# Cross-attention's scores laid out by key, their maxima taken from one turned block and handed round through DRAM

## The chip, the cores and the metric

The kernel runs on one core of a Trainium2 chip. A core has five engines that run their own instruction streams: TensorE (matrix products into PSUM, and transposes, which are products with an identity), VectorE, ScalarE, GpSimd and SyncE, which here only starts transfers. They share SBUF (128 partitions) and PSUM (eight banks of 2 KB per partition), and wait for each other through semaphores. The metric is device time in microseconds: the median of plain runs. The profile is of a separate, single execution of the same kernel.

## The reference

One decoder layer in float32: 32 sequences of 112 tokens, width 256, 16 heads of 16. Three residual steps: windowed causal self-attention, cross-attention to 375 context vectors with a bias that depends on the distance of key and query, and a mixture of eight experts of which each token takes two. The step that the change touches:

```python
q = (hidden_states @ Wq).reshape(B, S, H, D).transpose(0, 2, 1, 3)      # S = 112
kv = (key_value_states @ Wkv).reshape(B, K, 2, H, D)                    # K = 375
scores = jnp.einsum('bhsd,bhkd->bhsk', q, k)
rel = jnp.arange(K)[None, :] - jnp.arange(S)[:, None]
bias = rel_bias[_relative_position_bucket(rel)].transpose(2, 0, 1)[None]
attn = jax.nn.softmax(scores + bias, axis=-1)
out = jnp.einsum('bhsk,bhkd->bshd', attn, v).reshape(B, S, E)
return out @ Wo
```

The softmax subtracts each row's maximum over the 375 keys before the exponential. The sum that it divides by comes for free: the values carry a column of ones, so the product with the weights yields it too.

## The kernel before

**Slots.** Sequences go in eight groups of four. Everything up to the experts is cut into steps, and a table puts each step in a numbered slot. Slots 20 to 147 hold one cross item each, (group, sequence, quarter of the heads): four heads at a time, one per block of 32 partitions of the array. Slots 24 to 119 also hold one self item; the lead-in (slots 0 to 16) holds self items in pairs, and slots 120 to 147 cross items alone. The loop from line 1226 emits a slot: first `scores` of its item, then `average` of items three slots back, then `weigh` of the item two slots back, mixed with the steps due (projections of keys, values and queries, norms, routing), then the late ones (`divide`, `turn`, `attended`).

**Order.** `IN_ORDER` (line 51) names the engines whose instructions keep the written order: TensorE, VectorE, ScalarE. GpSimd's order is written out by `pool_order`. SyncE's is left to the scheduler. So an instruction that waits holds up all that is written behind it on its engine.

**One cross item.** `scores` (L464): per head block one product, queries as weights (32x112), keys moving (375 columns), into one of four PSUM banks (L477); self scores beside it (L488). VectorE adds the bias or mask and takes each row's minimum of the negated sum in the same instruction (L503, with a short read of the accumulator behind each). GpSimd subtracts the row's minimum (L509). `weigh` (L515), two slots later: twelve transposes (three chunks of 125 keys, four heads) bring the weights key-first (L530), and ScalarE takes the exponential out of PSUM (L531), one call per chunk. Self items take four transposes and one call. `average` (L533) multiplies by the values (L554). PSUM: four banks for scores, two for transposes, two for projections and the rest.

**Transfers.** SyncE loads each sequence's context (L434, two buffers, which at the start serve the bias table too: `hot` and `by_rel`), spreads the bias (L293 to L298: a small product, a store of `by_rel` to DRAM, and a load of 112 shifted copies), blanks the experts' row store in 28 pieces during the first 28 cross slots (L740, each held until that slot's scores are under way), stores results (L769) and loads x (L111). GpSimd starts the indirect transfers of the experts (L725, L962, L949, L1044). `first_plan` and `later_plan` (L909, L917) lay out the experts' tiles on VectorE, with small operations on tensors in SBUF such as L853 to L863.

Of the kernel before, what the change touches and what calls it, by code (L numbers as in the profile page):

```python
# [11 lines left out]
F32 = mybir.dt.float32  # L12
# [26 lines left out]
NWARM = 24  # L39
LAG = 4  # L40
# [10 lines left out]
IN_ORDER = {mybir.EngineType.PE, mybir.EngineType.DVE, mybir.EngineType.Activation}  # L51
# [27 lines left out]
def decoder_kernel(  # L79
# [95 lines left out]
    with ExitStack() as att, ExitStack() as own_att:  # L175
# [112 lines left out]
        bias = wpool.tile([S, H, K], F32, name="bias")  # L288

        def spread_bias():  # L290
# [6 lines left out]
            nc.sync.dma_start(by_rel_d, by_rel)  # L297
            nc.sync.dma_start(  # L298
                bias,
                bass.AP(  # L300
                    tensor=by_rel_d.tensor, offset=by_rel_d.offset,
                    ap=[[1, S], [NREL, H], [1, K]],
# [122 lines left out]
        def cross_queries(g, c):  # L425
            if c == 0:
                cross_q[g] = two.tile([P, NC2, 2, GT], F32, tag="q_cross", name=f"q_cross{g}")
            ps = ps_pj.tile([P, GT], F32, tag="pj", name=f"q2ps{g}_{c}")
            project(ps, wq_sb[:, :, c * P:(c + 1) * P], normed[g, 2][1])
            by_parity(cross_q[g][:, c], ps, g == 0)  # L430

        def load_context(g, b):
            ct = two.tile([P, NC2, K], F32, tag="ct", name=f"ct{g}_{b}")
            nc.sync.dma_start(ct, ctx_t[g * GB + b].rearrange("(c p) k -> p c k", p=P))  # L434
# [28 lines left out]

        def scores(cross, selfs):  # L464

            name = "_".join(str(v) for part in (cross or (), *selfs) for v in part)
            w = two.tile([S, 4, K + S], F32, tag="w", name=f"w{name}", bufs=3)
            low = small.tile([S, 3, 4], F32, tag="low", name=f"low{name}")
            at = K if cross else 0
            sc = [ps_sc.tile([S, 512], F32, tag="sc", name=f"sc{name}_{r}") for r in range(4)]  # L470
            if cross:
                g, b, s = cross
                c, p = divmod(s, 2)
                kT, q = keys[g, b][1], cross_q[g]
                for r in range(4):
                    rows = slice(32 * r, 32 * r + 32)
                    scored[cross] = nc.tensor.matmul(  # L477
                        sc[r][:, :K], q[rows, c, p, b * S:(b + 1) * S], kT[rows, c, :],
                        start=True, stop=True,
                    ).ins  # L480
            if selfs:
                g, b, s = selfs[0]
                c, p = divmod(s, 2)
                n, at_b = len(selfs), slice(b * S, (b + 1) * S)
                q, k = self_in[g, c]
                for r in range(4):
                    rows = slice(32 * r, 32 * r + 32)
                    nc.tensor.matmul(  # L488
                        sc[r][:, at:at + n * S].rearrange("q (p k) -> q p k", p=n),
                        q[rows, at_b], k[rows, p:p + n, at_b], start=True, stop=True,  # L490
                    )
            spans = []
            if cross:
# [831 lines left out]
```

## Time and profile before

| | us |
|---|---|
| median of plain runs (3 runs) | 1262.01 (1261.37 to 1262.40) |
| profiled execution, its own time | 1270.69 |
| span of that execution, first to last instruction | 1269.0 |
| first and last cross scores (L477) in it | 84.8 and 879.1 |
| TensorE busy in 300 to 400 us | 99.23 of 100 |
| VectorE, ScalarE, GpSimd busy there | 62.72, 54.10, 73.49 of 100 |

In a group line, the columns are line, engine, operation, output and inputs by name, shapes, count; after the first bar busy time in us and the mean ns of one; after the second the engine's idle time ahead of them and what ended it. In an order-of-time line: start and duration in us, then the instruction, a count where several follow without a gap (the duration then covers them all), and idle time before it in brackets. A transfer line ends with KB each and the median us from issue to landing. A float32 product is recorded as two instructions, a transpose as one. The table of stretches gives for each stretch its length and each engine's busy us.

### The profile page before, as it was taken

To read this page: it belongs to the slowest core of one execution; us is meant where nothing else is said; L and a number is where in the kernel's file an instruction comes from. 1 tells how busy PE (TensorE), PEld (TensorE's weight loads), DVE (VectorE), ACT (ScalarE), POOL (GpSimd) and SP (SyncE) were. 2 spreads that over 40 slices of the span, in tenths; PEclk is the share of its full clock that TensorE was granted. 3 is DMA by queue.
4 is the path that set the end of the run, shared out by engine and by line. 5 is a ranking of instruction groups with operands and counts; after the bars stand their busy time and mean duration, and the time that the engine had idled before them with its cause. 6 is when DMAs were issued, how large, how long until landed. Compare 5 with 4: busy or idle time off the path is not lost.

```text
span 1269.0 us, 29648 instructions
## 1 busy us (share of the span) xinstructions
PE 1227.4 (97%) x11648; PEld 972.5 (77%) x11648; DVE 651.0 (51%) x3012; ACT 570.1 (45%) x1201; POOL 839.0 (66%) x784
## 2 busy tenths in 40 slices
PE   9999999999999999999999999998789999999997
PEld 6666776777787787778778777766678898888886
DVE  5653654665566566557566665665325323332221
ACT  4454554555556456555555545454222222222222
POOL 8545664577767777767776796687556655665552
PEclk9999999999999999999999999999889999999999
DMA  8129876731100200200110020130366778888882
GB/s 229 34 69 197 203 169 161 180 87 42 44 26 14 73 14 14 74 24 15 39 33 26 14 59 26 36 128 25 115 209 195 212 208 276 239 234 244 244 247 30
DMA packets 70204, 143.00 MB, mean 113 GB/s; under 512 B 5521, under 2 KB 60498, under 8 KB 65074
## 3 DMA queue, kind: packets, MB, share of 16 engines
q0 software_dynamic: 20784, 85.92, 23.1%
q1 hardware_dynamic: 49282, 55.20, 17.3%
q8 instruction: 92, 1.51, 0.5%
q14 instruction: 46, 0.38, 0.1%
HBM read 90.88 MB, written 50.21 MB: 111 GB/s over the span
## 4 chain that ended last, share of the span: by engine, by line
PE 92%; ACT 2%; DVE 2%; POOL 1%; issue 1%; another core or an unknown queue 1%; DMA 0%; POOLq 0%; ACTq 0%; DVEq 0%
PE gu L1018 18%; PE wT L530 14%; PE py L1037 9%; PE sc L477 8%; PE k2ps L383 6%; PE v2ps L450 6%; PE avc_s L554 6%; PE ops L597 4%; PE ctrwT L530 3%; PE sc L488 3%; PE vps L416 2%; PE qps L383 2%; PE q2ps L383 2%; PE kps L383 2%; PE tp L377 1%; ACT wT L531 1%
## 5 line engine op out<-in xcount | busy, mean ns | idle before, releaser
L509 POOL TENSOR_TENSOR w<-w,low 112x448 f32<-112x448 f32 (+1 forms) x256 | 459.4, 1814 | 211.1 <-DVE low L503 210.1
L503 DVE CUSTOM_DVE_ANT_0 w<-sc,bias 112x375 f32<-112x375 f32 x512 | 270.4, 542 | 118.2 <-PE sc L488 96.2
L531 ACT ACTIVATE wT<-wT 125x448 f32<-125x448 f32 (+1 forms) x394 | 199.0, 542 | 100.7 <-PE wT L530 94.3
L1018 PE MATMUL gu<-xT,w 128*128 128x256 f32 (+1 forms) x1248 | 229.9, 342 | 1.9 <-issue 1.9
L530 PEld LDWEIGHTS wT<-ident,w 112*125 112x125 f32 (+1 forms) x1576 | 187.6, 174 | 46.1 <-issue 14.2
L1018 PEld LDWEIGHTS gu<-xT,w 128*128 128x128 f32 x1248 | 202.1, 192 | 26.8 <-issue 5.7
L530 PE MATMUL wT<-ident,w 112*125 112x112 f32 (+1 forms) x1576 | 216.0, 275 | 5.8 <-ACT wT L531 5.8
L1026 DVE SCALAR_TENSOR_TENSOR hid<-gu,w,sil 128x256 f32<-128x256 f32 (+1 forms) x156 | 67.2, 432 | 233.6 <-ACT sil L1023 228.2
L1044 POOL DMA_INDIRECT out_dram<-y,to x63 | 100.4, 1594 | 111.8 <-ACT y L1043 94.2
L1023 ACT ACTIVATE sil<-gu,w 128x256 f32<-128x256 f32 (+1 forms) x156 | 67.5, 433 | 147.4 <-PE gu L1018 131.9
L503 DVE CUSTOM_DVE_ANT_0 w<-sc,wmask 112x112 f32<-112x112 f32 x512 | 129.0, 268 | 2.6 <-PE sc L488 2.6
L477 PE MATMUL sc<-kT,q_cross 32*112 32x375 f32 x1024 | 123.3, 518 | 1.3 <-DVE low L503 1.0
L1037 PE MATMUL py<-w,hid 128*128 128x256 f32 x504 | 116.8, 383 | 0.4 <-DVE x L767 0.4
L1037 PEld LDWEIGHTS py<-w,hid 128*128 128x128 f32 x504 | 94.0, 193 | 12.1 <-DVE x L767 0.6
L450 PE MATMUL v2ps<-wkv_sb,ct 128*125 128x256 f32 x384 | 94.3, 381 | 0.0
L383 PE MATMUL k2ps<-ct,wkv_sb 128*128 128x375 f32 x256 | 92.3, 483 | 0.0
L503 DVE DVE_READ_ACCUMULATOR2_ANT low<- 112x1 f32 x1024 | 84.0, 82 | 0.0
L602 DVE TENSOR_TENSOR x<-x,ops 112x256 f32<-112x256 f32 x64 | 24.8, 418 | 111.1 <-PE ops L597 110.9
L1043 ACT ACTIVATE y<-py,gate 128x256 f32<-128x256 f32 x63 | 27.2, 471 | 108.6 <-PE py L1037 106.8
L725 POOL DMA_INDIRECT xslots<-xn,to x64 | 61.8, 966 | 19.7 <-issue 14.8
L962 POOL DMA_INDIRECT xg<-xslots,rows_i x63 | 60.7, 963 | 18.9 <-issue 17.4
L450 PEld LDWEIGHTS v2ps<-wkv_sb,ct 128*125 128x125 f32 x384 | 67.2, 188 | 7.7 <-DVE q_cross L389 0.5
(208 smaller groups left out, 1646.6 us busy)
## 6 DMA issues: line engine op xcount, KB each, us to landing
xslots<-zeros SPq DMA_DIRECT2D x28, 1060.0 KB, 7.6
ct<-in_ctx_t_dram SPq DMA_DIRECT2D x32, 375.0 KB, 3.3
x<-in_x_dram SPq DMA_DIRECT2D x8, 448.0 KB, 6.6
out_dram<-x SPq DMA_DIRECT2D x8, 448.0 KB, 3.2
bias<-by_rel_d SPq DMA_DIRECT2D x1, 2625.0 KB
xslots<-xn,to POOLq DMA_INDIRECT x64
xg<-xslots,rows_i POOLq DMA_INDIRECT x63
out_dram<-y,to POOLq DMA_INDIRECT x63
```

What stands on the lines that cost most here:

```text
L383: nc.tensor.matmul(ps, w[:, k, :], xT[:, k, :], start=(k == 0), stop=(k == NC2 - 1))
L450: nc.tensor.matmul(ps[:, i, :], ct[:, k, j * KC:(j + 1) * KC], wkv_sb[:, k, D:2 * D], start=(k == 0), stop=(k == NC2 - 1),)
L477: scored[cross] = nc.tensor.matmul(sc[r][:, :K], q[rows, c, p, b * S:(b + 1) * S], kT[rows, c, :], start=True, stop=True,).ins
L503: nc.vector.tensor_tensor_reduce(out=w[:, r, lo:hi], in0=sc[r][:, lo:hi], in1=add, scale=-1.0, scalar=FAR, op0=ALU.add, op1=ALU.min, accum ...
L509: nc.gpsimd.tensor_tensor(w[:, :, lo:hi], w[:, :, lo:hi], low[:, i].unsqueeze(2).to_broadcast([S, 4, hi - lo]), op=ALU.subtract,)
L530: nc.tensor.transpose(tp[:m, r, :], w[:, r, lo:lo + m], ident[:S, :S])
L531: nc.scalar.activation(wT[:m, j], tp[:m], AF.Exp, scale=-1.0)
L554: nc.tensor.matmul(av[32 * r:32 * r + 32, i, p, :], v, x, start=(j == 0), stop=(j == n - 1),)
L1018: nc.tensor.matmul(ps[:, m, :st], w[:, lo:lo + P], xT[:, c, :st], start=(c == 0), stop=(c == NC2 - 1),)
L1023: nc.scalar.activation(sil[:, :st], ps[:, 0, :st], AF.Silu, bias=w[:, bias_at + f:bias_at + f + 1])
L1037: nc.tensor.matmul(py[:, h, :], hid[:, f, h * P:(h + 1) * P], w[:, lo:lo + D], start=(f == 0), stop=(f == NFC - 1),)
L1044: added = nc.gpsimd.indirect_dma_start(out=out, out_offset=row_of(to[:, h:h + 1]), in_=y[:, h, :], in_offset=None, compute_op=ALU.add,)
```

## The change

Cross scores are computed transposed: keys as weights (three chunks of 32x125), queries moving (112 columns), twelve products instead of four. They come out key-first, in the layout in which `average` wants the weights, so the weights themselves are no longer transposed. The bias is loaded in the matching layout, 125 rows. VectorE adds it without taking a minimum.

The maximum over keys now runs across partitions. VectorE takes the larger of the three chunks, elementwise (`most`). At the head of the next slot `maxima` transposes that one block (four transposes), VectorE reduces it from PSUM to 112x4 maxima, SyncE stores these to DRAM and loads them back to all 125 partitions. A slot later `lessen` subtracts them on GpSimd, and a slot after that `exps` takes one exponential in place. Self items keep their way. `average` moves one slot later, except in the lead-in, and with it the last routing and plan.

Context loads and blanking stores go from SyncE's queue to ScalarE's. SyncE joins the engines in written order. Cross queries are held in one buffer per half of the width. Core of the diff:

```diff
-IN_ORDER = {mybir.EngineType.PE, mybir.EngineType.DVE, mybir.EngineType.Activation}
+IN_ORDER = {
+    mybir.EngineType.PE, mybir.EngineType.DVE, mybir.EngineType.Activation, mybir.EngineType.SP
+}
...
-        bias = wpool.tile([S, H, K], F32, name="bias")
+        bias = wpool.tile([KC, H, NKC, KC], F32, name="bias")
...
+            n = (NKC - 1) * KC + S
             nc.sync.dma_start(
-                bias,
+                bias.rearrange("k h j q -> k h (j q)")[:, :, :n],
                 bass.AP(
                     tensor=by_rel_d.tensor, offset=by_rel_d.offset,
-                    ap=[[1, S], [NREL, H], [1, K]],
+                    ap=[[1, KC], [NREL, H], [1, n]],
...
-            nc.sync.dma_start(ct, ctx_t[g * GB + b].rearrange("(c p) k -> p c k", p=P))
+            nc.scalar.dma_start(ct, ctx_t[g * GB + b].rearrange("(c p) k -> p c k", p=P))
...
-                for r in range(4):
-                    rows = slice(32 * r, 32 * r + 32)
-                    scored[cross] = nc.tensor.matmul(
-                        sc[r][:, :K], q[rows, c, p, b * S:(b + 1) * S], kT[rows, c, :],
-                        start=True, stop=True,
-                    ).ins
+                for j in range(NKC):
+                    for r in range(4):
+                        rows = slice(32 * r, 32 * r + 32)
+                        scored[cross] = nc.tensor.matmul(
+                            sc[r][:KC, j * S:(j + 1) * S], kT[rows, c, j * KC:(j + 1) * KC],
+                            q[rows, p, b * S:(b + 1) * S], start=True, stop=True,
+                        ).ins
...
             for r in range(4):
+                if cross:
+                    c, p = divmod(cross[2], 2)
+                    nc.vector.tensor_tensor(
+                        t[:, r], sc[r][:KC, :at].rearrange("k (j q) -> k j q", j=NKC),
+                        bias[:, 8 * c + 2 * r + p, :, :S], op=ALU.add,
+                    )
+                for i in range(n):
+                    lo = i * S
                     nc.vector.tensor_tensor_reduce(
-                        out=w[:, r, lo:hi], in0=sc[r][:, lo:hi], in1=add,
+                        out=w[:, r, lo:lo + S], in0=sc[r][:S, at + lo:at + lo + S], in1=wmask,
                         scale=-1.0, scalar=FAR, op0=ALU.add, op1=ALU.min,
                         accum_out=low[:, i, r:r + 1],
                     )
+            if cross:
+                most = two.tile([KC, 4, S], F32, tag="most", name=f"most{name}")
+                nc.vector.tensor_tensor(most, t[:, :, 0, :], t[:, :, 1, :], op=ALU.max)
+                nc.vector.tensor_tensor(most, most, t[:, :, 2, :], op=ALU.max)
+                shown[cross] = t, most
+            for i in range(n):
+                part = w[:, :, i * S:(i + 1) * S]
                 nc.gpsimd.tensor_tensor(
-                    w[:, :, lo:hi], w[:, :, lo:hi],
-                    low[:, i].unsqueeze(2).to_broadcast([S, 4, hi - lo]), op=ALU.subtract,
+                    part, part, low[:, i].unsqueeze(2).to_broadcast([S, 4, S]), op=ALU.subtract
                 )
...
+        def maxima(cross):
+            t, most = shown[cross]
+            name = "_".join(str(v) for v in cross)
+            tp = ps_tr.tile([S, 4, KC], F32, tag="tr", name=f"mtr{name}")
+            for r in range(4):
+                nc.tensor.transpose(tp[:, r, :], most[:, r, :], ident[:KC, :KC])
+            top = small.tile([S, 4], F32, tag="top_w", name=f"top_w{name}")
+            nc.vector.tensor_reduce(top, tp, AX.X, ALU.max)
+            top_d = dram.tile([4, S], F32, name=f"top_d{name}")
+            nc.sync.dma_start(top_d.rearrange("r q -> q r"), top)
+            spread = two.tile([KC, 4, S], F32, tag="spread", name=f"spread{name}")
+            nc.sync.dma_start(
+                spread.rearrange("k r q -> k (r q)"),
+                bass.AP(
+                    tensor=top_d.tensor, offset=top_d.offset, ap=[[0, KC], [1, 4 * S]],
+                ),
+            )
+            shown[cross] = t, spread
+
+        def lessen(cross):
+            t, spread = shown[cross]
+            nc.gpsimd.tensor_tensor(
+                t, t, spread.unsqueeze(2).to_broadcast([KC, 4, NKC, S]), op=ALU.subtract
+            )
+
+        def exps(cross):
+            t, _ = shown.pop(cross)
+            t = t.rearrange("k r j q -> k (r j q)")
+            nc.scalar.activation(t, t, AF.Exp)
...
-            filled = nc.sync.dma_start(part, zeros.unsqueeze(1).to_broadcast([P, n // P, ROW]))
+            filled = nc.scalar.dma_start(part, zeros.unsqueeze(1).to_broadcast([P, n // P, ROW]))
...
-                        slot = slot_of[kind, g, b, 2 * half + 1] + 3
+                        lead_in = kind == "s" and g < 2
+                        slot = slot_of[kind, g, b, 2 * half + 1] + (3 if lead_in else 4)
...
-        put_route(NG - 1, base[NG] + 5, base[NG] + 8)
-        free_self, free_all = base[NG - 1], base[NG] + 5
-        plan_at = {base[EARLY + 1] - 1: first_plan, base[NG] + 14: later_plan}
+        put_route(NG - 1, base[NG] + 6, base[NG] + 9)
+        free_self, free_all = base[NG - 1], base[NG] + 6
+        plan_at = {base[EARLY + 1] - 1: first_plan, base[NG] + 15: later_plan}
...
+                for i, fn in ((1, maxima), (2, lessen), (3, exps)):
+                    if cross := items.get(slot - i, (None,))[0]:
+                        do(partial(fn, cross))
                 if slot in items:
                     made[slot] = scores(*items[slot])
```

## The prediction

> **What bounds the kernel.** I read the page's totals first, then the stretch table, then the groups with shapes apart, then the order of time in one slot.
>
> ```profile
> PE 1227.4 (97%) x11648; PEld 972.5 (77%) x11648; DVE 651.0 (51%) x3012; ACT 570.1 (45%) x1201; POOL 839.0 (66%) x784
> ```
> ```profile
> core 0: us, PE busy (x) PEld busy (x) DVE busy (x) ACT busy (x) POOL busy (x), PEclk, DMA share, GB/s
> 300.00:400.00 100.00, 99.23 (x1165) 77.11 (x1165) 62.72 (x308) 54.10 (x112) 73.49 (x67) 1.00 0.11 32
> ```
>
> In attention TensorE has no gap (99.23 of 100), so removed TensorE work could pay in full. But VectorE is at 62.7 and GpSimd at 73.5 of 100, and the change gives VectorE more. The groups, mean ns second to last before the bar:
>
> ```profile
> L509 POOL TENSOR_TENSOR w<-w,low 112x1500 f32<-112x1500 f32 x128 | 344.7, 2693 | 207.1 <-DVE low L503 206.2 <-issue 0.5
> L503 DVE CUSTOM_DVE_ANT_0 w<-sc,bias 112x375 f32<-112x375 f32 x512 | 270.4, 542 | 118.2 <-PE sc L488 96.2 <-PE sc L477 17.0 <-issue 4.5
> ...
> L530 PE MATMUL wT<-ident,w 112*125 112x112 f32 x1152 | 166.7, 281 | 5.8 <-ACT wT L531 5.8
> ...
> L509 POOL TENSOR_TENSOR w<-w,low 112x448 f32<-112x448 f32 x128 | 118.8, 934 | 4.0 <-DVE low L503 3.9
> ```
>
> Then two score blocks of TensorE in order of time:
>
> ```profile
> 405.67 0.90 PE L477 MATMUL sc<-kT,q_cross 32*112 32x375 f32 x8
> 406.39 0.37 PE L488 MATMUL sc<-k_self,q_self 32*112 32x112 f32 x8
> 406.69 1.12 PE L530 MATMUL wT<-ident,w 112*125 112x112 f32 x8
> 407.65 1.44 PE L383 MATMUL k2ps<-ct,wkv_sb 128*128 128x375 f32 x4
> ...
> 410.60 0.90 PE L477 MATMUL sc<-kT,q_cross 32*112 32x375 f32 x8
> ```
>
> From start to start: cross scores 0.72 us, self scores 0.30, eight transposes 0.96 (0.12 each), this slot 4.93. The same starts through one group of 16 slots (298.3 plus, period 105.9 us) give 7.36, 4.93, 10.94, 4.63, 10.19, 4.16, 8.01, 6.36, 7.17, 4.94, 6.67, 4.63, 7.16, 4.93, 7.36, 6.50. **Short and long slots alternate**, and that decides what the saving is worth.
>
> **The change on TensorE, per slot.** Twelve cross transposes become four: −8×0.12 = −0.96. The four are of 125 columns, not 112: +0.05. Scores: 12 matmuls of 112 columns instead of 4 of 375. The self row has the shape (32 rows, 112 columns): 4 of them take 0.30, three times that is 0.90, against 0.72: +0.18; weights of 125 columns may add 0.08. Net −0.66 (ends −0.75, −0.55). If nothing else moved: 127 slots × 0.66 = −84 us.
>
> **VectorE, per slot with self scores.** Start-to-start prices. Before, one pair (cross 0.47, self 0.19) is 0.66, four are 2.64. Now the add has 336 columns and no accumulator: 0.47−39×1.04 ns = 0.43; four pairs 2.46. New: two maxima of 448 elements. The near row is the rank comparison of 112x256, both inputs in SBUF (424 ns, so N plus 151 cycles at 1.04 ns each): 0.62, and the second needs the first: 1.29 together. New too: a reduction of 500 elements from PSUM, 0.67. Sum +1.8 us, on VectorE's other 1.35 us per slot (the busy time left of each slot without line 503).
>
> What matters more is a **loop** that was not there: the transposes of the maxima come first in TensorE's next slot and wait for the second maximum, and that slot's scores stand behind them. From score start to next score start: VectorE starts 1.35 us in (before: scores at 410.60, first cross add at 411.71, 1.11 us; plus 0.24 for the longer scores), then 2.46, 1.29, 0.1 to wake TensorE, 0.5 for four transposes: **5.7 us**. Six of the 16 slots leave TensorE less than 5.7.
>
> **The port.** Both inputs of the maxima lie in SBUF, and the trace has such an operation beside GpSimd's subtraction:
>
> ```profile
> 814.81 0.23 DVE L856 TENSOR_TENSOR own<-index_p,begins 128x80 f32<-128x80 f32 x1
> 814.96 2.65 DVE L859 TENSOR_TENSOR shift_by<-region,behind 128x8 f32<-128x8 f32 x1
> 817.54 0.15 DVE L862 TENSOR_TENSOR rest_by<-have,behind 128x8 f32<-128x8 f32 x1
> ```
> ```profile
> 814.82 2.78 POOL L509 TENSOR_TENSOR w<-w,low 112x1500 f32<-112x1500 f32 x1 [3.68 <-DVE low L503]
> ```
>
> Eight elements took 2.65 us, to GpSimd's end at 817.60, where its twin takes 0.15; the adds of line 503 (one input PSUM) keep 542 ns beside the same GpSimd work. Now GpSimd's self subtraction is released by the last self score, the very moment the first maximum starts; it gets in between the two maxima, since the second must wait for the first. The second then waits 0.9 (row of 934 ns): loop **6.6**. [...] I take the row, because the gap between the maxima is there every time; bounds 0 and 2.4 (the large subtraction instead).
>
> **Sum for the 96 slots with self scores**, each the larger of its own length −0.66 and the loop, added over their measured lengths: +40 us at 6.6, −7 at 5.7. Beyond it, between the last maximum and the next add there is room for 1.29 us of VectorE's other work (0.1+0.5+1.35−0.67); four slots in 16 have 2.1 to 2.3 (norm statistics, transposes of averages, residual adds), 0.9 over, 3.6 per 16: +21. I take 0.9 of both: **+55**.
>
> **The 31 others.** Loop 1.05+4×0.43+1.29+0.6 = 4.65, TensorE −0.66: sum −1; 5.1 (a port wait of 0.45, as the large subtraction falls in it now and then) +8; 5.6 +19. I take **+8**.
>
> **The bounce through DRAM.**
>
> ```profile
> xslots<-zeros SPq DMA_DIRECT2D x28, 1060.0 KB, 7.6
> ct<-in_ctx_t_dram SPq DMA_DIRECT2D x32, 375.0 KB, 3.3
> ...
> out_dram<-x SPq DMA_DIRECT2D x8, 448.0 KB, 3.2
> ...
> by_rel_d<-by_rel SPq DMA_DIRECT2D x1, 30.4 KB, 6.9
> ```
>
> The maxima leave in 448 packets of 4 bytes; the row of 448 packets (each 1 KB) lands in 3.2. Spread: 125 packets of 1792 bytes. From ct (16 packets per engine) to the fills (64): 4.3/48 = 0.09 us per packet, rest 1.86. Over 16 engines 2.6 us. [...] No transfer before has 125 rows. [...] SyncE, now in written order, waits out the first landing; behind it only loads and stores due slots later. GpSimd waits ahead of the self subtraction, needed two slots on.
>
> **ScalarE.** Three exponentials of 448 (0.49 each) become one of 1344 (about 1.3): nothing gained. It issues 60 DMAs (0.37 to 0.6 each, 24 us of its 46% idle): hidden. One is not: the second context load reuses by_rel's buffer, and now stands in ScalarE's order in slot 0 ahead of the projection's copy.
>
> ```profile
> 15.74 0.34 SPq L297 DMA_DIRECT2D by_rel_d<-by_rel  x1
> ...
> 17.20 0.54 ACT L397 ACTIVATE q_self<-qps 128x448 f32<-128x448 f32 x1 [3.16 <-PE qps L383]
> ```
>
> The store lands at 22.6: **+5**. [...] The tail's averages, last routing and plan come a slot later, with expert tiles to fill it: 0 to +5, **+2**.
>
> Sum +55+8+5+2 = +70 on the profiled span of 1269.0 (1270.7 with what lies around it). The median of plain runs is 1262.0, 0.7% less; I put the same 70 on it: **1332**.
>
> **Rivals.**
> 1. *The port hardly bites* (GpSimd waits). [...] Against: line 859. Self slots −7+9, start and tail +7: **1272**, 1252 to 1292.
> 2. *The bounce sets the pace.* For: 6.9 us for by_rel's store under load, 4-byte packets. Two slots plus about 1.5 must hold 0.5+0.67+chain+2.43: at a chain of 12, 7.1 us per slot; +75 with self, +60 without: about **1400**. [...]
> 3. *Faster.* VectorE's loop under about 5.4 us in every self slot: no port wait, and adds at 0.33 as the 256-element residual adds do. At 5.2: −25 −5 +7: **1239**; all of the saving, 1185, needs loops under 3.5.
>
> **Chances.** Forecast 0.60 (own range 1296 to 1366), rival 1 0.17, 2 0.12, 3 0.11. The range leaves most of rival 3 below and rival 2's upper half above: 1254 to 1394. Within 0.2% (2.5 us, what a measurement can tell) only rival 1 and 3 overlap: 0.03. Faster 0.11, slower 0.86.
>
> **What would show it.** Right: the second maximum far above 0.62 us, TensorE's waits ahead of the turned maxima put down to VectorE, short slots at 6 us or more, line 859's pattern 96 times. Wrong: maxima near 0.62 with TensorE at 99 of 100 (rival 3), or the subtraction waiting on the spread and the exponentials on it (rival 2).

## The result

The changed kernel takes **1921.96 us** (median of 4 runs, 1920.92 to 1939.83), the kernel before 1261.69 beside it: a ratio of **1.527** (95% interval 1.518 to 1.536). The direction was as forecast; the size was not: +660 us, where 1332 (+70) and a range up to 1394 were given.

In the profiled executions the span grew by 650.7 us (1269.0 to 1919.7). From the first cross scores to the last, which took 795.1 us before, it is now 1425.0 (92.5 to 1517.4): +630. The start is 7.7 us longer, the part after the last scores 13.2. So nearly all of it is lost slot by slot, 128 times.

### The profile page after: what moved, and what is told of

Same layout as the page of the kernel before. It is cut to its first block, busy times and chain, and to the rows that moved or that the text cites. A ratio compares the mean times of both kernels' runs of the same rounds, so it can differ in the third digit from the quotient of the medians.

```text
span 1919.7 us, 32039 instructions
## 1 busy us (share of the span) xinstructions
PE 1314.3 (68%) x12672; PEld 1008.6 (53%) x12672; DVE 951.6 (50%) x2884; ACT 538.9 (28%) x945; POOL 909.6 (47%) x784
## 4 chain that ended last, share of the span: by engine, by line
DMA 48%; PE 30%; DVE 9%; POOL 7%; issue 4%; ACT 1%; SPq 1%; ACTq 0%; POOLq 0%; DVEq 0%
DMA top_d<-top_w 31%; DMA spread<-top_d 15%; PE gu L1066 11%; PE py L1085 6%; POOL t L555 5%; DVE t L510 2%; PE ops L645 2%; PE sc L491 1%; PE k2ps L388 1%; DVE most L523 1%; DVE most L524 1%; PE mtr L539 1%; PE str L578 1%; DVE top_w L541 1%; PE sc L503 1%
## 5 line engine op out<-in xcount | busy, mean ns | idle before, releaser
L555 POOL TENSOR_TENSOR t<-t,spread 125x1344 f32<-125x1344 f32 x128 | 391.9, 3062 | 775.5 <-DMA spread<-top_d 653.7
L562 ACT ACTIVATE t<-t 125x1344 f32<-125x1344 f32 x128 | 169.4, 1323 | 871.4 <-POOL t L555 866.6
L539 PE MATMUL mtr<-ident,most 125*112 125x125 f32 x512 | 98.5, 327 | 269.1 <-DVE most L524 254.1
L510 DVE TENSOR_TENSOR t<-sc,bias 125x336 f32<-125x336 f32 x512 | 248.8, 502 | 40.5 <-PE sc L503 33.7
L491 PE MATMUL sc<-q_cross,kT 32*125 32x112 f32 x3072 | 148.9, 335 | 0.0
L524 DVE TENSOR_TENSOR most<-most,t 125x448 f32<-125x448 f32 x128 | 140.1, 1095 | 4.4
L491 PEld LDWEIGHTS sc<-q_cross,kT 32*125 32x125 f32 x3072 | 122.3, 230 | 29.3 <-issue 29.3
L523 DVE TENSOR_TENSOR most<-t 125x448 f32<-125x448 f32 x128 | 119.6, 934 | 1.1
L602 PE MATMUL avc_s<-t,v_cross 125*32 125x112 f32 x2304 | 90.4, 321 | 30.0 <-ACT t L562 21.3
L528 POOL TENSOR_TENSOR w<-w,low 112x448 f32<-112x448 f32 x96 | 102.5, 1068 | 3.8 <-DVE low L516 3.8
```

Of the source, the lines that this page charges most:

```text
L491: scored[cross] = nc.tensor.matmul(sc[r][:KC, j * S:(j + 1) * S], kT[rows, c, j * KC:(j + 1) * KC], q[rows, p, b * S:(b + 1) * S], start=T ...
L510: nc.vector.tensor_tensor(t[:, r], sc[r][:KC, :at].rearrange("k (j q) -> k j q", j=NKC), bias[:, 8 * c + 2 * r + p, :, :S], op=ALU.add,)
L523: nc.vector.tensor_tensor(most, t[:, :, 0, :], t[:, :, 1, :], op=ALU.max)
L524: nc.vector.tensor_tensor(most, most, t[:, :, 2, :], op=ALU.max)
L539: nc.tensor.transpose(tp[:, r, :], most[:, r, :], ident[:KC, :KC])
L555: nc.gpsimd.tensor_tensor(t, t, spread.unsqueeze(2).to_broadcast([KC, 4, NKC, S]), op=ALU.subtract)
```

## The profile after

First the totals, one stretch deep in attention (its columns: length, busy us of TensorE's products, its weight loads, VectorE, ScalarE, GpSimd, then granted clock, transfer share, GB/s), and the chain that ended last.

```profile
PE 1314.3 (68%) x12672; PEld 1008.6 (53%) x12672; DVE 951.6 (50%) x2884; ACT 538.9 (28%) x945; POOL 909.6 (47%) x784
```
```profile
core 0: us, PE busy (x) PEld busy (x) DVE busy (x) ACT busy (x) POOL busy (x), PEclk, DMA share, GB/s
800.00:1000.00 200.00, 131.68 (x1592) 97.70 (x1592) 124.24 (x367) 66.91 (x111) 105.77 (x83) 0.81 0.28 42
```
```profile
DMA 48%; PE 30%; DVE 9%; POOL 7%; issue 4%; ACT 1%; SPq 1%; ACTq 0%; POOLq 0%; DVEq 0%
DMA top_d<-top_w 31%; DMA spread<-top_d 15%; PE gu L1066 11%; PE py L1085 6%; POOL t L555 5%; DVE t L510 2%; PE ops L645 2%; PE sc L491 1%; PE k2ps L388 1%; DVE most L523 1%; DVE most L524 1%; PE mtr L539 1%; PE str L578 1%; DVE top_w L541 1%; PE sc L503 1%
```

TensorE, at 99.2% in attention before, is at 66%, and no engine is above 66%. Almost half of the chain is two transfers: the store of the 448 maxima (31% of the span) and the load that spreads them (15%). The groups of instructions say who waited for these:

```profile
L555 POOL TENSOR_TENSOR t<-t,spread 125x1344 f32<-125x1344 f32 x128 | 391.9, 3062 | 775.5 <-DMA spread<-top_d 653.7
L562 ACT ACTIVATE t<-t 125x1344 f32<-125x1344 f32 x128 | 169.4, 1323 | 871.4 <-POOL t L555 866.6
L539 PE MATMUL mtr<-ident,most 125*112 125x125 f32 x512 | 98.5, 327 | 269.1 <-DVE most L524 254.1
...
L524 DVE TENSOR_TENSOR most<-most,t 125x448 f32<-125x448 f32 x128 | 140.1, 1095 | 4.4
...
L523 DVE TENSOR_TENSOR most<-t 125x448 f32<-125x448 f32 x128 | 119.6, 934 | 1.1
```

GpSimd idled 653.7 us on the spread, ScalarE 866.6 us on GpSimd's subtraction, with copies for TensorE behind it in its written order. TensorE waited 254.1 us for the second maximum (L524), which takes 1095 ns on the average and the first 934, where their medians, 626 and 622, are what two chained maxima take alone. So VectorE's loop and its slowed maxima, which the prediction had, are there, but most of the chain is the bounce, for which its sum has no term. SyncE's own waits and order of time show how it runs:

```profile
SPq L545 <- DMA top_d<-top_w: 1242.7, 126, 17.9
...
SPq L543 <- DVE top_w L541: 143.4, 31, 76.2
```
```profile
898.70 0.27 SPq L545 DMA_DIRECT2D spread<-top_d  x1
899.01 0.32 SPq L817 DMA_DIRECT2D out_dram<-x  x1
899.37 0.49 SPq L543 DMA_DIRECT2D top_d<-top_w  x1
910.45 0.27 SPq L545 DMA_DIRECT2D spread<-top_d  x1
910.76 0.32 SPq L543 DMA_DIRECT2D top_d<-top_w  x1
919.86 0.27 SPq L545 DMA_DIRECT2D spread<-top_d  x1
```

SyncE issues a store, stands 9 to 11 us until it has landed, issues the spread, and only then, 0.3 us later, the next item's store. In what follows the 128 cross items are counted from 0, so that item 28 is that of slot 48. From issue of the store to issue of the spread it is 9.3 us (median of items 28 to 100; mean 9.6), and the slot there is 10.44 us (mean from reduction to reduction): **the store's landing, once per slot, is nearly the whole slot.** While the blanking stores run beside it (items 4 to 28) the landing takes 13.7 on the average and the slot 14.96. In items 28 to 100 a finished row of maxima waits 3.0 us for SyncE on the average; the spread takes 6.5 (median where it releases the subtraction).

## The experiments

Diffs are against the changed kernel unless another is named. Where no interval is given, the time is of a single run; ratios are to the kernel before on the same chip. On these chips it took 1261 to 1274 us, so a difference in us between runs of different chips can be off by 1%; the runs from the reduction on are on the slower ones.

### The bounce taken out

```diff
+        nothing = wpool.tile([KC, 4, S], F32, name="nothing")
+        nc.gpsimd.memset(nothing, 0.0)
...
-            top_d = dram.tile([4, S], F32, name=f"top_d{name}")
-            nc.sync.dma_start(top_d.rearrange("r q -> q r"), top)
-            spread = two.tile([KC, 4, S], F32, tag="spread", name=f"spread{name}")
-            nc.sync.dma_start(...)
-            shown[cross] = t, spread
+            shown[cross] = t, nothing
```

> Left out: the store of the maxima to DRAM and the load back; a constant tile of zeros is subtracted in their place, so the exponentials are of the plain scores. The maxima are still formed, turned and reduced, the subtraction and all lags stay. Theory A (the bounce sets the pace, by the latency of its two transfers within the two slots that are given to it): with it gone what is left is what the prediction summed, VectorE's loop with the port wait, about 1332 us, and 1300 to 1370 counts for it. Theory B (the pace is set by VectorE's longer loop and its port waits, the transfers only follow): 1800 us or more, since nothing of that is taken away.

1607.42 us, ratio 1.275 (1.271 to 1.279). The bounce is worth 315 of the 660. But +346 are left with no transfer in the way, five times what was forecast. Groups, then the two maxima of one slot beside GpSimd in order of time:

```profile
L548 POOL TENSOR_TENSOR t<-t,nothing 125x1344 f32<-125x1344 f32 x128 | 388.0, 3033 | 9.2 <-DVE most L526 8.8
...
L525 DVE TENSOR_TENSOR most<-t 125x448 f32<-125x448 f32 x128 | 201.2, 1572 | 1.1
L526 DVE TENSOR_TENSOR most<-most,t 125x448 f32<-125x448 f32 x128 | 177.0, 1383 | 4.4
```
```profile
817.15 2.60 DVE L525 TENSOR_TENSOR most<-t 125x448 f32<-125x448 f32 x1
819.78 1.24 DVE L526 TENSOR_TENSOR most<-most,t 125x448 f32<-125x448 f32 x1
```
```profile
816.25 3.02 POOL L548 TENSOR_TENSOR t<-t,nothing 125x1344 f32<-125x1344 f32 x1
819.22 1.32 POOL L530 TENSOR_TENSOR w<-w,low 112x448 f32<-112x448 f32 x1
```

The first maximum meets the large subtraction and ends 0.48 us behind it, the second meets the self subtraction and ends 0.48 us behind that. On the average the two take 3.0 us per slot, from the start of the first to the end of the second, instead of 1.28 alone.

### No maximum at all

```diff
-                most = two.tile([KC, 4, S], F32, tag="most", name=f"most{name}")
-                nc.vector.tensor_tensor(most, t[:, :, 0, :], t[:, :, 1, :], op=ALU.max)
-                nc.vector.tensor_tensor(most, most, t[:, :, 2, :], op=ALU.max)
-                shown[cross] = t, most
+                shown[cross] = t, None
...
-                for i, fn in ((1, maxima), (2, lessen), (3, exps)):
+                for i, fn in ((3, exps),):
```

> Left out: all that has to do with the maximum of the cross scores (the two elementwise maxima, the four transposes, the reduction, the bounce and GpSimd's subtraction); exponentials are of the plain scores, a slot's place for them unchanged. What stays is the layout by key alone. By the prediction's terms TensorE is the bound again: 1262 - 84 (twelve transposes become four, dearer scores) - 128 x 0.53 (these four too) + 5 (start) = about 1115 us. If the layout by key is itself slow (scores of 24 short products dearer than 0.9 us, a late average, ScalarE's queue), it stays above 1200.

1147.53 us, ratio **0.910** (0.908 to 0.913), faster than both. It leaves out the cross maximum: the exponentials are of the scores plus bias themselves, which is the same softmax as long as none overflows. From first to last scores it takes 656 us of TensorE's time in 678.8. So the new layout pays, and the way in which the maxima are found and handed round costs 774 us on top of it.

### A spread over all sixteen transfer engines

```diff
-            spread = two.tile([KC, 4, S], F32, tag="spread", name=f"spread{name}")
+            spread = two.tile([P, 4, S], F32, tag="spread", name=f"spread{name}")
...
-                    tensor=top_d.tensor, offset=top_d.offset, ap=[[0, KC], [1, 4 * S]],
+                    tensor=top_d.tensor, offset=top_d.offset, ap=[[0, P], [1, 4 * S]],
```

> The load of the maxima fills 128 partitions instead of 125, all else as in the changed kernel. Theory A1 (the load is slow since it runs on 5 of 16 engines, 2 us of data, and the next store waits behind it in the same queue): data time falls to 0.7 us, store and load each land 1 to 2 us sooner, the two slots given shrink by 2 to 4 us together, so 1 to 2 us per slot: 1670 to 1800 us. Theory A2 (the 448 packets of 4 bytes of the store are what is slow, wherever they stand): 1880 to 1925 us.

1958.87 us in a single run: no better, and inside neither range. The spread itself went from 6.5 to 5.0 us, but the store took 10.4. In the changed kernel the transfer view of 913 to 914 us, when only the spread moves, shows its queue at 31.6% of 16 engines, which is five of them:

```profile
q1 hardware_dynamic: 68, 0.12, 31.6%
```

So the five engines are real, and they are not what costs. The spread is not what the slot waits for.

### The store in rows of 16 bytes

The maxima are kept query first in DRAM, so each partition's four go as one packet: 112 of 16 bytes instead of 448 of 4. GpSimd reads the spread with a stride of four.

```diff
-            top_d = dram.tile([4, S], F32, name=f"top_d{name}")
-            nc.sync.dma_start(top_d.rearrange("r q -> q r"), top)
-            spread = two.tile([KC, 4, S], F32, tag="spread", name=f"spread{name}")
+            top_d = dram.tile([S, 4], F32, name=f"top_d{name}")
+            nc.sync.dma_start(top_d, top)
+            spread = two.tile([KC, S, 4], F32, tag="spread", name=f"spread{name}")
...
-            shown[cross] = t, spread
+            shown[cross] = t, spread.rearrange("k q r -> k r q")
```

> The maxima are stored query by query, 112 packets of 16 bytes instead of 448 of 4, and read back in that order; GpSimd reads them with a stride of four. All else as in the changed kernel. Theory A2 (number of packets): the store lands in about 4 us instead of 9.4, chain 5 us shorter, 2.5 us less per slot if the two slots' latency binds: about 1600 us; 1350 to 1450 if SyncE's waiting for each landing binds. Theory A1 (the store waits behind the load on 5 engines): the landing falls by 1 us or less, 1800 to 1900 us.

1587.37 us in a single run: the same 1792 bytes, 335 us less, and no longer slower than the kernel without any bounce. SyncE's waits and order of time:

```profile
SPq L543 <- DVE top_w L541: 757.7, 116, 77.2
SPq L545 <- DMA top_d<-top_w: 319.7, 128, 9.6
```
```profile
916.75 0.30 SPq L543 DMA_DIRECT2D top_d<-top_w  x1
918.30 0.26 SPq L545 DMA_DIRECT2D spread<-top_d  x1
930.12 0.30 SPq L543 DMA_DIRECT2D top_d<-top_w  x1
931.55 0.26 SPq L545 DMA_DIRECT2D spread<-top_d  x1
```

The landing falls from 9.3 to 1.56 us (median), the spread from 6.5 to 4.5, and SyncE now waits mostly for VectorE's maxima instead of its own stores. The subtraction, reading with a stride, takes 3.73 us instead of 3.06:

```profile
L555 POOL TENSOR_TENSOR t<-t,spread 125x1344 f32<-125x1344 f32 x128 | 477.0, 3727 | 137.5 <-DMA spread<-top_d 116.1
```

So, on balance, all of the bounce's cost goes with the 4-byte store. It is a balance: the wait for the spread also moves the subtraction, so that the maxima meet it less than without the bounce (2.66 us against 3.0).

### One reduction instead of two maxima

Against the kernel of 16-byte rows: a reduction reads one tensor where each maximum reads two.

```diff
-                nc.vector.tensor_tensor(most, t[:, :, 0, :], t[:, :, 1, :], op=ALU.max)
-                nc.vector.tensor_tensor(most, most, t[:, :, 2, :], op=ALU.max)
+                nc.vector.tensor_reduce(most, t.rearrange("k r j q -> k r q j"), AX.X, ALU.max)
```

> The store of rows16, and the two elementwise maxima (both inputs in SBUF) replaced by one reduction over the three chunks, which has one input. Theory P (the maxima wait for GpSimd because they read two tensors from SBUF; 2.6 to 2.9 us per slot in rows16 where 1.28 is their own time): the reduction takes (1344+151)/0.96 GHz = 1.56 us whatever GpSimd does, 1.1 to 1.3 us less per slot, 140 to 165 us: 1420 to 1450. Against P (GpSimd slows any work of VectorE on SBUF): the reduction waits too, and its own 0.28 more costs 36 us: about 1620.

1478.35 us, ratio 1.161 (1.156 to 1.166), where two maxima gave 1.259; 109 us less, though not the 137 to 167 that theory P forecast.

```profile
L523 DVE TENSOR_REDUCE most<-t 125x448 f32<-125x1344 f32 x128 | 216.2, 1689 | 1.1
```

The reduction took 1.68 to 1.70 us in every slot, whatever GpSimd did; the 1.56 expected is an estimate at the 1.04 ns an element of line 503 before (542 ns at 375, 268 at 112). Alone, two maxima (1.28) would be cheaper; beside GpSimd they took 2.66. VectorE's slot fell from 8.73 to 7.80, and 128 times 0.93 is 119 us; the attention part fell by 117. The gain is one for one.

### The turned maxima behind the scores, and both together

Against the kernel of 16-byte rows:

```diff
-                for i, fn in ((1, maxima), (2, lessen), (3, exps)):
+                for i, fn in ((2, lessen), (3, exps)):
...
                     made[slot] = scores(*items[slot])
+                if cross := items.get(slot - 1, (None,))[0]:
+                    do(partial(maxima, cross))
```

> The store of rows16, and the maxima of the item before are turned and reduced behind this slot's scores instead of ahead of them. Theory L (the loop: the turned maxima stand at the head of TensorE's slot and hold the next scores back until VectorE has its second maximum, so VectorE idles 1.8 us per slot while TensorE turns and scores): most of that idle time goes, 1.0 to 1.5 us per slot, 130 to 190 us: 1400 to 1460. Without L (VectorE's own work and the port set the pace): less than 40 us gained, 1550 to 1590.

1577.08 us in a single run, ratio 1.239 where 1.259 was before the move, which is in the range given for theory L failing. The attention part is 35 us shorter, the part behind it 25 us longer. That the turned maxima stand ahead of the scores is little of what the loop costs: moved behind them, VectorE still idles 2.0 us of an 8.51 us slot (1.82 of 8.73 before the move). With the reduction as well:

> rows16_reduce and rows16_late together. P and L both right: VectorE per slot 2.27 adds and self scores, 1.56 reduction of chunks, 1.16 other work, 0.66 reduction, some 0.5 idle, 6.15 us, a little under the 6.25 of before: 1587 - 155 - 160 = about 1270, 1230 to 1320. If only one of them holds, 1400 to 1450.

1491.52 us, ratio 1.169 (1.163 to 1.175): the intervals overlap with those of the reduction alone. The move is worth nothing there, and the forecast of 1230 to 1320 was far off.

### No bounce and no subtraction

Against the kernel without the bounce; `lessen` goes too, so GpSimd's large instruction is gone and the exponentials are of the plain scores, while maxima are still found, turned and reduced.

```diff
-                for i, fn in ((1, maxima), (2, lessen), (3, exps)):
+                for i, fn in ((1, maxima), (3, exps)):
```

> As no_bounce (no bounce, exponentials of the plain scores), and GpSimd's large subtraction is left out too; VectorE's and TensorE's work is unchanged. Theory P: in no_bounce the maxima take 3.00 us per slot, 1.72 over their own; only the self subtraction (0.93, 96 slots) is left to get in their way, so 0.7 of it remains, 1.0 us per slot less, 130 us: about 1480. If the surplus is not GpSimd's: 1590 to 1610.

1405.38 us in a single run, ratio 1.104, well below the 1480 of theory P. An instruction of GpSimd, which holds 1% of the chain in the kernel without the bounce, cost 202 us there, or 17% of the kernel before. Of the 1.61 us by which the mean slot falls, 1.26 are the maxima and 0.30 other operations of VectorE (among them the rank comparison, which also reads two tensors in SBUF, falls from 3.2 us to 0.43 in the median):

```profile
L526 DVE TENSOR_TENSOR most<-most,t 125x448 f32<-125x448 f32 x128 | 138.8, 1084 | 4.4
...
L525 DVE TENSOR_TENSOR most<-t 125x448 f32<-125x448 f32 x128 | 79.5, 621 | 1.1
```

The first maximum is back at 621 ns, its own price, and the second at 1084 on the average: 1.24 wherever a self subtraction starts between the two (96 slots), 0.62 elsewhere. That is the pattern that the prediction described. But +132 us to the kernel before are left, with the maxima at 1.74 us. The kernel's totals, TensorE's wait for the second maximum, and VectorE and then TensorE in the seam of two slots, in order of time:

```profile
PE 1202.5 (86%) x12672; PEld 947.7 (68%) x12672; DVE 907.0 (65%) x2884; ACT 546.4 (39%) x945; POOL 533.0 (38%) x657
...
L541 PE MATMUL mtr<-ident,most 125*112 125x125 f32 x512 | 87.6, 299 | 154.5 <-DVE most L526 132.2
```
```profile
814.59 1.24 DVE L526 TENSOR_TENSOR most<-most,t 125x448 f32<-125x448 f32 x1
815.75 0.17 DVE L717 TENSOR_REDUCE tot<-pr 112x4 f32<-112x32 f32 x1
816.28 0.18 DVE L719 RECIPROCAL tot<-tot 112x4 f32<-112x4 f32 x1 [0.35 <-POOL tot L718]
816.62 0.68 DVE L543 TENSOR_REDUCE top_w<-mtr 112x4 f32<-112x500 f32 x1 [0.17 <-PE mtr L541]
817.72 0.51 DVE L512 TENSOR_TENSOR t<-sc,bias 125x336 f32<-125x336 f32 x1 [0.42 <-PE sc L505]
```
```profile
815.98 0.61 PE L541 MATMUL mtr<-ident,most 125*112 125x125 f32 x4 [1.30 <-DVE tot L717]
816.52 0.92 PE L493 MATMUL sc<-q_cross,kT 32*125 32x112 f32 x24
```

TensorE waits 1.30 us for VectorE to finish the slot, then VectorE waits in three pieces (0.94) while TensorE turns and scores. They take turns.

### The store on ScalarE's queue

With 4-byte packets as in the changed kernel, but SyncE no longer has the next store behind the spread's wait.

```diff
-            nc.sync.dma_start(top_d.rearrange("r q -> q r"), top)
+            nc.scalar.dma_start(top_d.rearrange("r q -> q r"), top)
```

> The changed kernel with one difference: the store of the maxima (448 packets of 4 bytes) is issued from ScalarE's queue, the load back stays on SyncE's. Theory Q (SyncE waits out each store's landing, 9.4 us, before it may issue the next pair, so a slot can't be shorter than a landing): stores of two items now overlap, SyncE waits only for what is left, and the pace becomes that of rows16, 8.7 us per slot: 1590 to 1700. Theory C (the chain's latency must fit into two slots: 0.5 + 0.67 + 9.4 + 0.3 + 6.5 + 3.05, over 2 is 10.2 per slot): nothing gained, 1850 to 1930.

1791.77 us in a single run. Some 130 of the 335 us that 16-byte rows give come with the queue alone; the landing is still 8.3 us (14.7 beside the blanking stores), a finished row no longer waits for its queue (0.03 us), and items 28 to 100 take 9.7 each. Neither account of the bounce is whole: the packets make a landing of 8 to 10 us, and in SyncE's queue one comes after another. With the queue away, theory C's sum with this run's landing of 8.3 and spread of 6.0 gives 9.4 us, an estimate close to the 9.7. For the changed kernel that sum gave 10.2 against 10.44, so there the queue and the chain of two slots bind at nearly the same pace, and this run does not part them fully. It isn't a clean test either, for ScalarE now waits for the reduction ahead of each store.

### Products that keep TensorE busy

Against the kernel with 16-byte rows and the reduction; the three added products are overwritten.

```diff
             tp = ps_tr.tile([S, 4, KC], F32, tag="tr", name=f"mtr{name}")
+            for _ in range(3):
+                nc.tensor.matmul(tp[:, 0, :], ident[:, :S], ident[:, :KC], start=True, stop=True)
```

> rows16_reduce with three products of the identity with itself (112x125, float32) ahead of each turn of the maxima, where TensorE otherwise waits: work for nothing, 0.75 us per slot. Theory K (TensorE's waits lower its granted clock, 0.91 there, and the slower products lengthen the long slots): the clock rises to 0.96 or more, TensorE's other products return to their times of before, and the total falls, 1420 to 1470. Without K: the clock changes little or does not matter, and in about half of the slots the 0.75 us add up, 1500 to 1540.

1472.27 us in a single run, against 1478.35. The mean granted clock rises from 0.908 to 0.929, short of the 0.96 that theory K asked for, and the time is nearly the same. Whether the work added was hidden in TensorE's waits or paid for by the clock, and how much of the whole loss the lower clock makes, this cannot tell.

### One chunk instead of a maximum over three

Against the kernel without bounce and subtraction: the first chunk is turned and reduced in place of the largest, so VectorE loses the two maxima and nothing else goes.

```diff
-                most = two.tile([KC, 4, S], F32, tag="most", name=f"most{name}")
-                nc.vector.tensor_tensor(most, t[:, :, 0, :], t[:, :, 1, :], op=ALU.max)
-                nc.vector.tensor_tensor(most, most, t[:, :, 2, :], op=ALU.max)
-                shown[cross] = t, most
+                shown[cross] = t, t[:, :, 0, :]
```

> As no_bounce_nosub (no bounce, no large subtraction, exponentials of the plain scores), and the two elementwise maxima are left out: the first chunk alone is turned and reduced. So 1.74 us of VectorE per slot go and nothing else. Theory V (VectorE's time in the loop with TensorE sets the pace, microsecond for microsecond): 1405 - 128 x 1.74 = 1183, but not below TensorE's own work, no_max's 1147 plus four transposes of 0.5 per slot, so 1200 to 1230. Theory W (what is left is the wait for the turned block at the head of the slot, however short VectorE is): 1300 or more.

1216.2 us in a single run, ratio 0.955, as theory V had it: 189 us for taking 1.74 us per slot from an engine that was idle for a fifth of the attention part. Totals:

```profile
PE 1146.0 (94%) x12672; PEld 897.0 (74%) x12672; DVE 695.6 (57%) x2628; ACT 546.3 (45%) x945; POOL 501.1 (41%) x657
```

TensorE is at 94% again, with the transposes of a block, the reduction and the loop still there. So what costs is how much VectorE does in the loop, and not that there is a loop.

### The fastest one with the old queues and places

Against the kernel without a maximum, three changes at once: context loads back on SyncE, exponentials one slot after the scores, averages, routing and plan where they were.

```diff
-            nc.scalar.dma_start(ct, ctx_t[g * GB + b].rearrange("(c p) k -> p c k", p=P))
+            nc.sync.dma_start(ct, ctx_t[g * GB + b].rearrange("(c p) k -> p c k", p=P))
...
-                        lead_in = kind == "s" and g < 2
-                        slot = slot_of[kind, g, b, 2 * half + 1] + (3 if lead_in else 4)
+                        slot = slot_of[kind, g, b, 2 * half + 1] + 3
...
-                for i, fn in ((3, exps),):
+                for i, fn in ((1, exps),):
```

> As no_max (the maximum of the cross scores is left out), with the context loads back on SyncE's queue, the exponentials one slot behind the scores, and averages, last routing and plan back in their slots of before. By the prediction's term for the start (ScalarE waits for by_rel's store) the first cross scores come 5 to 8 us sooner, near 85 us; the tail gives 0 to 10: 1130 to 1145. If the start's wait was hidden, 1145 to 1150.

1165.28 us, ratio 0.913 (0.909 to 0.917), beside 0.910 (0.908 to 0.913): no gain, where 1130 to 1145 was expected. ScalarE's copy in the start no longer waits, as the lines from the changed kernel and then from this one show, and the first cross scores come at 88.3 us instead of 92.8 (84.8 before). But the attention part is 690 us instead of 679, and what follows it 386 instead of 373; why was not tested.

```profile
22.98 0.54 ACT L402 ACTIVATE q_self<-qps 128x448 f32<-128x448 f32 x1 [8.83 <-DMA ct<-in_ctx_t_dram]
```
```profile
17.45 0.55 ACT L402 ACTIVATE q_self<-qps 128x448 f32<-128x448 f32 x1 [3.16 <-PE qps L388]
```

### The steps in one table

Each kernel in shares of the kernel before on its own chip; each adds one part to the row above.

| kernel | ratio | step |
|---|---|---|
| new layout, no maximum | 0.910 | −9.0% |
| + one block turned and reduced | 0.955 | +4.5 |
| + maximum over three chunks | 1.104 | +14.9 |
| + GpSimd's subtraction | 1.275 | +17.1 |
| + bounce: the changed kernel | 1.527 | +25.2 |

The second and third are single runs; a few tenths of a per cent there say nothing.

## Why the prediction was wrong

**What bounds the kernel, and TensorE's part: right.** TensorE's busy time between first and last scores fell from 781.5 to 699.5 us with one block still turned, −82, where −84 was forecast; the attention part fell by 57. The match is in part luck: the 24 short products were charged 0.90 us and took 0.74 (median, start to start), 20 us less over all slots, and something that the sum doesn't have took as much more.

**The bounce: the step that failed most.** Its store was priced at 3.2 us by the row of 448 packets. Those are of 1 KB, these of 4 bytes, and the count of packets was the wrong likeness: measured 9.3, and 13.7 beside the blanking stores. The other near row, the store of `by_rel` at 6.9 us, was quoted and used for rival 2 alone. Then the step "SyncE, now in written order, waits out the first landing; behind it only loads and stores due slots later" overlooked what is due in the very next slot: the next item's store. With that, a landing is not a latency that two slots cover but a stretch of SyncE's time in each slot; in the changed kernel SyncE waited for its stores 1242.7 us, and the bounce, which has no term in the sum, cost 315. Spread (6.5 against the 2.6 estimated over 16 engines) and subtraction (3.06 against 2.43, an estimate from the rows of 934 ns at 448 elements and 2693 at 1500) were under-priced too, and neither decides. The spread's 125 rows moved on five engines (31.6% of 16); with 128 rows it took 5.0 us, 1.5 less, of a transfer that wasn't the bound.

**Rival 2 had this transfer, but not the queue**, at a chance of 0.12 and with 1400. Its inequality spreads the chain over two slots and has no queue. With the measured store of 9.3 and spread of 6.5 it gives (0.5 + 0.67 + 15.8 + 3.06 − 1.5) / 2 = 9.3 us per slot, against 10.44 measured. So 12 us was too small a chain, which is most of what it missed; the rest is what a finished row waits for SyncE. The sign that the prediction named for it, the subtraction waiting on the spread and the exponentials on the subtraction, is what the profile shows (653.7 and 866.6 us).

**The wait for GpSimd: right in kind; the size holds by luck.** What the two engines share, the prediction's "port", no run shows; that each of the two maxima ended 0.48 us behind a subtraction of GpSimd's, the lines of the slot without the bounce do. A maximum alone took the 0.62 us charged (at 1.04 ns an element, which the 542 ns at 375 elements and 268 at 112 of line 503 before give as well). For the collision 0.9 us was charged, by the row of line 859. Measured are 0.62 for the second maximum beside the self subtraction (1.24 instead of 0.62), and, without the bounce, 3.0 instead of 1.28 for both on the average: 1.7, twice the charge. The bound of 2.4, "the large subtraction instead", was named and not taken: the first maximum, when it met that subtraction, took 2.60 us. The row was rightly taken over the bound of 0: GpSimd does get in between the two maxima, in 96 slots without the large subtraction. In the changed kernel, where the subtraction waits for the spread, they meet less often: 2.07 us, 0.79 over 1.28, which is the mean of the 0.9 and 0.45 charged. But in 75 of the 128 slots nothing collides, and in the others it is mostly the large subtraction that does; the number came out because the bounce had stretched the slots.

**The loop: the sum was wrong in form.** This step and the wait for GpSimd are the +346 us that are left without the bounce, where +70 was forecast. For each slot the larger of TensorE's own length less 0.66 and a loop of VectorE's was taken, with 1.29 us of room for VectorE's other work. The runs answer with a slot that grows by almost all that VectorE gets (means over 127 slots; the maxima from the start of the first to the end of the second, or the reduction in their place):

| VectorE's share of a mean slot, us | adds, self | maxima | reduction | other | idle | slot | TensorE busy |
|---|---|---|---|---|---|---|---|
| no bounce | 2.27 | 3.00 | 0.66 | 1.39 | 1.55 | 8.87 | 6.24 |
| 16-byte rows | 2.27 | 2.66 | 0.67 | 1.31 | 1.82 | 8.73 | 6.33 |
| 16-byte rows, reduction | 2.28 | 1.69 | 0.67 | 1.30 | 1.86 | 7.80 | 6.04 |
| no bounce, no subtraction | 2.28 | 1.74 | 0.66 | 1.09 | 1.49 | 7.26 | 5.92 |
| the same, one chunk | 2.28 | 0 | 0.66 | 1.19 | 1.67 | 5.80 | 5.49 |
| the changed kernel | 2.27 | 2.07 | 0.67 | 1.12 | 5.15 | 11.28 | 6.81 |

In the first four rows, none of which has a 4-byte store, VectorE's idle time stays at 1.5 to 1.9 us whatever the maxima take: its work and a stretch in which it waits add up, and there is no room in which other work hides. The last 1.74 us came back as 1.46 per slot (186 of attention over 128). Idle time alone does not show why: with one chunk it is 1.67, and there TensorE, busy for 95% of the slot, is the bound. But in the first four rows TensorE idles too, 1.3 to 2.6 us per slot, mostly for the maxima, and both idle at once only 0.05 to 0.24 us: the two engines take turns. Which of VectorE's waits (for output products before the residual adds, 65 to 91 us in all; for turned blocks, 40 to 58; for scores, 40 to 54) keeps it so is not shown. The head of the slot, which the prediction singled out, is not it alone.

**Small terms.** The start: +5 forecast, +7.7 measured, 5.8 of it by the wait named (ScalarE's copy at 22.98 instead of 17.20). The tail: +2 forecast, +13 measured. Adds with one PSUM input kept one price (at most 510 ns) in every kernel, whatever GpSimd did, as said; with the self scores they came to 2.27 us per slot, where 2.46 was charged.

**Open.** Why a store of 4-byte packets lands so late (9.3 us); how much the lower granted clock (0.82, against 0.993 before), for which the prediction had no term, adds to each step (TensorE's busy time for the same products is 5.49 us per slot with one chunk and 5.92 with the maxima, so by this estimate up to 0.43 of the 1.46 may be the clock); how the bounce and the rest share the 660 us, since the order in which parts are taken away changes their steps.

## What to carry to other kernels

Price a small transfer by the size of its packets as well as by their number (here 448 of 4 bytes landed in 9.3 us, 448 of 1 KB in 3.2), and ask of a queue in written order what stands behind each wait: if it is the next round of the same chain, the latency is paid once per round and nothing covers it, as with these 9.3 us of a slot of 10.44. Before giving more work to an engine with time to spare, see whether it takes turns with the engine that sets the pace; then what it gets is added to every slot, as 1.46 of the maxima's 1.74 us were here, and so is a collision with a third engine that nobody waits for (202 us here). And when a maximum has to be found across partitions, ask first what happens without it: the rest of this change was worth 9%.

## What the runs showed of the hardware

**Landing of small stores.** From issue to landing, with the spreads beside it: 448 packets of 4 bytes 9.3 us (median, the changed kernel), 112 of 16 bytes 1.56; in the kernel before, 448 of 1 KB 3.2. Most of the 9.3 isn't the moving: in the kernel with the wide spread a store was issued at 905.42, its small packets stood in the records from 908 to 910, none after, and the next instruction was released at 915.76, 5.7 us later. With 16-byte packets all small ones stood between 917 and 918 and the release followed at 918.30. Over items 28 to 100 the release follows the last small packet by 5.0 us in the changed kernel and by 0.58 with 16-byte packets (medians). So on SyncE's queue the wait behind the last packet, 5.0 us or 0.58, is not one fixed time; what it is made of no run here shows.

**A strided operand on GpSimd.** The same subtraction of 125x1344 took 3.06 us with the spread read in order and 3.73 with a stride of four elements.

**TensorE's granted clock.** Its mean beside TensorE's share of busy time: 0.993 at 97% (before), 0.988 at 94% (one chunk), 0.929 at 86% (no bounce and no subtraction), 0.82 at 68% (the changed kernel). The trace's records of the clock hold two values, 1.0 and 0.5: 0.5 for 20 us of the kernel before, 32 with one chunk, 691 in the changed kernel. What sets it no run shows. One shape shows what goes with it, the projection of keys before, and in the changed kernel:

```profile
L383 PE MATMUL k2ps<-ct,wkv_sb 128*128 128x375 f32 x256 | 92.3, 483 | 0.0
```
```profile
L388 PE MATMUL k2ps<-ct,wkv_sb 128*128 128x375 f32 x256 | 108.0, 549 | 0.3 <-issue 0.3
```

The mean of 549 ns hides two prices: the median is 480, and 43 of the 256 took over 700, up to 996.
